# Four graph layers on one core: the row ends of the attention layer on ScalarE, two tiles at a time, between head sums and denominators

## The chip, the cores and the metric

The kernel runs on one core of a Trainium2 chip. The time is the device time of one execution in microseconds, and the time before is the median of three runs. A profile is one further execution, recorded instruction by instruction. Engines are named as the profile names them: PE is TensorE's matmul stream and PEld its weight loads, DVE is VectorE, ACT is ScalarE, POOL is GpSimd, SP is SyncE, whose queue issues most loads.

## The reference, cut to what matters

Four layers follow each other on N = 2708 rows of F = 256 features with one dense matrix adj (2708 x 2708). Each is `x = layernorm(x + layer(x, adj))`. The change concerns the end of layer 1, a graph attention layer with four heads of 64 features:

```python
h = (x @ W).reshape(n, heads, head_dim)
e = src[:, :, None] + dst.T[None, :, :]          # one number per row, head and column
e = jnp.where(e > 0, e, ALPHA * e)
e = jnp.where(adj[:, None, :] > 0, e, NEG_INF)
attn = jax.nn.softmax(e, axis=-1)
out = jnp.einsum('nhm,mhd->nhd', attn, h).reshape(n, heads * head_dim)
mu, var = out.mean(-1), out.var(-1)
out = (out - mu) / jnp.sqrt(var + LN_EPS) * gamma + beta
x = layernorm(x + out)
```

Layer 2 starts from three numbers per row (attention logits of its three heads), a product of the new x with a 256 x 3 matrix. The rest of layer 2 and layer 3 are not touched.

## The kernel before

Rows are held in 22 tiles of 128 (the last has 20). Layer 1 goes through the rows in three groups, each of two segments: 8, 8 and 6 tiles, that is 1024, 1024 and 660 columns of transposed output. A group takes two passes, one for each pair of heads (`q`). A pass is a loop over 22 chunks `c` of 128 rows of the sum. For each chunk VectorE makes two weight tiles `p`, one per head (L665, the exponential of the logits as a maximum of products, times the mask); a pool of four `p` buffers lies between VectorE and TensorE. TensorE then sums on each segment the heads (`heads`, L647, 64-column matmuls of one head beside the other) into `acc`, and the denominators (`totals`, L656, 32-column matmuls) into `den`. Even chunks do heads and then denominators, odd chunks the reverse, so that two equal parts follow each other across a chunk's border. An fp32 matmul shows in the trace as two instructions. At the end of a pass ScalarE copies the two `acc` (L677) and the two halves of `den` (L681) to SBUF; four PSUM banks serve the three that a pass needs, so part of the next pass starts while those copies run.

The row ends of a group run during the two passes of the next one. `layer1_end` turns the sums of one tile into rows (three transposes, L570 and L571), adds beta to x on POOL (L573), divides by the denominators on VectorE (L578, L581, L583), and makes two layer norms with `moments`: bn_stats (L162), bn_aggr (L164), an addition (L166) and a power of -0.5 on POOL (L167), then L590 and L592 between the norms and L595 after the second. `layer1_logits` transposes the new x (L179), copies it to SBUF (L181), stores it through POOL's queue (L602), and multiplies it by the 256 x 3 matrix (L607), which ScalarE copies away (L610). These are generators, and `step(c)`, called at the end of every chunk, advances those begun: in pass 0 a new tile begins about every 2.7 chunks, and goes through the division and the first moments; in pass 1 every second chunk a tile goes through the rest.

The last group has no following passes. Its six row ends are mixed with the first sums of layer 2: `raw_sums` loads adjacency blocks through SP's queue (L256), combines them on VectorE (L296 to L299, and L275 to L278 once), and multiplies them (L309). One step of it follows each of the 13 steps of the row ends. Then come sums of the logits (L722), which need all of `u_all`, in a form that VectorE splits into `u_parts`.

What each engine executes is in order. The order is not simply that of the loops: a planner at build time estimates when each instruction could start, takes the order of the program as priority, and lets later instructions go ahead of ones that it thinks not ready. An instruction that waits on the chip holds up all that are behind it on its engine.

Of the kernel before, what the change touches and what calls it, by code (L numbers as in the profile page):

```python
# [9 lines left out]
F32 = mybir.dt.float32  # L10
# [9 lines left out]
P = 128  # L20
# [7 lines left out]
def kernel(  # L28
# [356 lines left out]
    if True:  # L385
# [13 lines left out]
        if True:  # L399
# [162 lines left out]
            if True:  # L562

                def layer1_end(pool, t, s, sums, dens):

                    n = sz(t)
                    at = (t - [lo for lo, hi in spans if hi > t][0]) * P
                    pt = ps_t.tile([P, 4, P], F32, tag="tr", name="tr")
                    for q in range(H // 2):
                        nc.tensor.transpose(pt[:n, q, :], sums[q][s][:, at : at + n], ident)  # L570
                    nc.tensor.transpose(pt[:n, H // 2, :], dens[s][:, at : at + n], ident)  # L571

                    nc.gpsimd.tensor_tensor(xs[t][:n], xs[t][:n], beta_b[:n], ALU.add)  # L573
                    yield
                    rden = small.tile([P, H // 2, 2], F32, tag="rdenh", name="rdenh")
                    totals = pt[:n, H // 2, :].rearrange("p (q i c) -> p q i c", i=2, c=CT)[:, :, :, CT - 1]
                    if s == 0:
                        nc.vector.reciprocal(rden[:n], totals)  # L578
                    else:
                        for q in range(H // 2):  # L580
                            nc.vector.reciprocal(rden[:n, q], totals[:, q ^ s])  # L581
                    o = pool.tile([P, F], F32, tag="o", name="o", bufs=len(ended))
                    nc.vector.tensor_tensor(  # L583
                        o[:n].rearrange("p (h d) -> p h d", d=HD),
                        pt[:n, : H // 2, :].rearrange("p q (i d) -> p (q i) d", d=HD),
                        rden[:n].rearrange("p q i -> p (q i)")[:, :, None].to_broadcast([n, H, HD]),
                        ALU.mult,
                    )
                    mean, rs = moments(o, n)
                    nc.vector.scalar_tensor_tensor(o[:n], o[:n], mean, gamma_b[:n], ALU.subtract, ALU.mult)  # L590
                    yield
                    nc.vector.scalar_tensor_tensor(o[:n], o[:n], rs, xs[t][:n], ALU.mult, ALU.add)  # L592
                    mean, rs = moments(o, n)
                    yield
                    nc.vector.tensor_scalar(xs[t][:n], o[:n], mean, rs, ALU.subtract, ALU.mult)  # L595

                def layer1_logits(pool, t):

                    n = sz(t)
                    xt = transposed(ps_t, pool, xs[t], n, "xt")  # L600
                    at, _, d = [p for p in xt_d if p[0] <= t * P][-1]
                    nc.gpsimd.dma_start(d[:, :, t * P - at : t * P - at + n], xt[:, :, :n])  # L602
                    yield

                    pm = ps_t.tile([P, 4, P], F32, tag="tr", name="pm")
                    for f in range(FC):
                        nc.tensor.matmul(  # L607
                            pm[:n, 0, :K], xt[:, f, :n], uw[:, f, :], start=(f == 0), stop=(f == FC - 1)
                        )
                    nc.scalar.copy(u_all[:n, t], pm[:n, 0, :K])  # L610
# [4 lines left out]
                for g in range(0, len(spans), 2):  # L615
# [9 lines left out]
                    def step(c):  # L625
# [4 lines left out]
                        if q == 0 and len(halves) < len(ended) and c > len(halves) * 8 // 3:  # L630
# [66 lines left out]
                for k in range(len(ended) + 7):  # L697
                    for i in range(len(ended)):
                        if 0 <= k - i < 4:
                            next(ends[i], None)  # L700
# [771 lines left out]
```

## Time and profile before

| quantity | us |
|---|---|
| median of 3 runs (lowest, highest) | 1925.73 (1924.24, 1928.12) |
| the profiled execution | 1929.04 |
| its span | 1927.3 |
| layer 1, group 1 (1024 columns, no row ends), pass 1 | 60.67 |
| group 2 (1024 columns, row ends of 8 tiles), passes 0 and 1 | 67.16 and 70.87 |
| group 3 (660 columns, row ends of 8 tiles), passes 0 and 1 | 50.05 and 55.27 |
| from there to the logits sums (row ends of 6 tiles) | 50.81 |

The passes are cut where ScalarE's copies of `den` start. A line of a window's answer gives start and end, the length, and then busy time with a count for PE, PEld, DVE, ACT and POOL, the granted clock of TensorE, the share of DMA time and GB/s. A line of a timeline gives start, length, engine, line, operation, written from read tiles, shapes and count, and in brackets how long the engine had been idle and what ended that. A line of the groups gives line, engine, operation and tiles, a count, busy time with the mean of one in ns, and the idle time before. The durations of neighbouring instructions on one engine overlap by up to about 0.1 us, so the distance from start to start is what an instruction costs in a row of them.

### The profile page before, as it was taken

The numbers are of one execution on the slowest core, as the hardware profiler recorded it, in microseconds if no ns is written. First come the engines' busy times: TensorE is split into PE (matmuls) and PEld (weight loads), VectorE is DVE, ScalarE is ACT, GpSimd is POOL, SyncE is SP. The second block draws the span as 40 slices with busy tenths as digits, with TensorE's granted clock in tenths as the row PEclk, the third lists the DMA queues.
The fourth block names the chain that finished last, engine by engine and source line by source line (L and its number), as shares of the span: only waits on it lengthen the run. The fifth ranks groups of instructions, "written<-read, shape, count | busy, mean of one in ns | idle before, by whom it ended". The sixth has DMA issues, their size and how long they took to land.

```text
span 1927.3 us, 22585 instructions
## 1 busy us (share of the span) xinstructions
PE 1864.0 (97%) x7475; PEld 1011.5 (52%) x7479; DVE 1316.4 (68%) x2409; ACT 617.2 (32%) x1064; POOL 261.2 (14%) x435
## 2 busy tenths in 40 slices
PE   8999989999999999999899999999999999999996
PEld 7788832222233778678444444444445555654444
DVE  4334368899898947455557889585877758855665
ACT  4444400000100103111355656455555555311001
POOL 1212110001112421000001000020200101211101
PEclk9999999999999999999999999999999999999998
DMA  8334400000000647555746656454554444643653
GB/s 294 123 143 159 155 23 1 2 28 9 15 1 23 157 103 194 141 131 121 206 137 187 182 163 174 121 158 112 148 155 127 116 114 124 186 115 97 197 152 101
DMA packets 432922, 235.90 MB, mean 122 GB/s; under 512 B 172150, under 2 KB 420620, under 8 KB 430364
## 3 DMA queue, kind: packets, MB, share of 16 engines
q1 hardware_dynamic: 416158, 207.40, 39.2%
q0 software_dynamic: 7760, 21.20, 3.5%
q10 hardware_dynamic: 8878, 5.76, 1.0%
q8 instruction: 62, 1.02, 0.2%
q14 instruction: 64, 0.52, 0.1%
HBM read 221.61 MB, written 12.65 MB: 122 GB/s over the span
## 4 chain that ended last, share of the span: by engine, by line
PE 80%; DMA 6%; DVE 6%; ACT 3%; issue 2%; SPq 2%; POOL 1%; ACTq 0%; DVEq 0%; POOLq 0%
PE m L309 38%; PE acc L647 10%; PE acc L203 7%; PE bank L1007 7%; PE den L656 5%; PE gate L882 4%; PE bank L983 3%; DMA strip<-in_adj_t_dram 2%; DVE p L665 2%; PE bank L1058 2%; SPq L256 1%; ACT below L452 1%; DVE p L1141 1%; PE pm L410 1%; POOL bn_rs L167 1%
## 5 line engine op out<-in xcount | busy, mean ns | idle before, releaser
L665 DVE SCALAR_TENSOR_TENSOR p<-fall_b,rise,mask 128x1024 f32<-128x1024 f32 (+1 forms) x264 | 297.7, 1150 | 27.1 <-PE den L656 14.6
L1137 ACT ACTIVATE p<-st,e_neg 128x1024 f32<-128x1024 f32 (+1 forms) x198 | 197.1, 1040 | 207.8 <-PE m L309 195.4
L309 PE MATMUL m<-s,xq 128*128 128x512 f32 (+3 forms) x660 | 230.3, 467 | 0.0
L647 PE MATMUL acc<-p,h 128*64 128x512 f32 (+2 forms) x1056 | 224.0, 556 | 3.0 <-DVE p L665 2.8
L203 PE MATMUL acc<-turn,strip 128*128 128x257 f32 (+1 forms) x836 | 191.6, 380 | 0.0
L309 PE MATMUL m<-p,xq 128*128 128x512 f32 (+1 forms) x396 | 183.9, 546 | 0.3 <-DVE p L297 0.3
L1140 ACT ACTIVATE p<-p 128x1024 f32<-128x1024 f32 (+1 forms) x198 | 178.8, 943 | 0.2
L309 PE MATMUL m<-p,x 128*128 128x512 f32 (+1 forms) x396 | 169.7, 547 | 5.1 <-DVE p L1141 4.8
L1141 DVE TENSOR_TENSOR p<-p,blk 128x1024 f32<-128x1024 f32 (+1 forms) x132 | 142.5, 1098 | 42.3 <-ACT p L1140 29.9
L296 DVE TENSOR_TENSOR s<-p 128x512 f32<-128x512 f32 (+1 forms) x132 | 83.1, 631 | 120.9 <-PE m L309 101.9
L203 PEld LDWEIGHTS acc<-turn,strip 128*128 128x128 f32 (+1 forms) x836 | 151.5, 185 | 25.3 <-issue 0.5
L309 PEld LDWEIGHTS m<-s,xq 128*128 128x128 f32 x660 | 124.7, 191 | 75.2 <-issue 58.9
L647 PEld LDWEIGHTS acc<-p,h 128*64 128x64 f32 x1056 | 65.5, 136 | 147.8 <-issue 117.5
L167 POOL TENSOR_TENSOR bn_rs<-bn_rs,neg_half 128x1 f32<-128x1 f32 (+1 forms) x110 | 81.8, 745 | 380.1 <-DVE bn_rs L166 373.2
L309 PE MATMUL m<-s,x 128*128 128x512 f32 (+3 forms) x330 | 127.2, 467 | 0.0
L656 PE MATMUL den<-p,h 128*32 128x512 f32 (+2 forms) x1056 | 124.1, 551 | 2.8 <-DVE p L665 2.7
L309 PEld LDWEIGHTS m<-p,x 128*128 128x128 f32 x396 | 74.9, 191 | 79.2 <-issue 61.1
L309 PEld LDWEIGHTS m<-p,xq 128*128 128x128 f32 x396 | 74.5, 190 | 77.8 <-issue 61.2
L452 ACT ACTIVATE below<-strip 128x384 bf16<-128x384 f32 x132 | 78.5, 594 | 72.6 <-DMA strip<-in_adj_t_dram 69.2
L1141 DVE TENSOR_TENSOR p<-p,turn 128x1024 f32<-128x1024 f32 (+1 forms) x66 | 71.6, 1107 | 21.4 <-ACT p L1140 13.3
L681 ACT COPY den<-den 64x512 f32<-64x512 f32 (+2 forms) x12 | 6.3, 529 | 249.2 <-PE den L656 249.1
L297 DVE TENSOR_TENSOR p<-p 128x512 f32<-128x512 f32 (+1 forms) x132 | 83.0, 629 | 1.7
(243 smaller groups left out, 2514.9 us busy)
## 6 DMA issues: line engine op xcount, KB each, us to landing
strip<-in_adj_t_dram SPq DMA_DIRECT2D x19, 1408.0 KB, 6.2
blk<-in_adj_t_dram SPq DMA_DIRECT2D x88, 256.0 KB, 3.4
blk<-in_adj_t_dram SPq DMA_DIRECT2D x88, 192.0 KB, 4.0
pa<-in_adj_t_dram SPq DMA_DIRECT2D x110, 128.0 KB, 2.7
turn<-in_adj_t_dram SPq DMA_DIRECT2D x44, 256.0 KB, 3.1
blk<-in_adj_t_dram SPq DMA_DIRECT2D x88, 128.0 KB, 2.5
p<-in_adj_t_dram SPq DMA_DIRECT2D x44, 256.0 KB, 3.5
turn<-in_adj_t_dram SPq DMA_DIRECT2D x44, 192.0 KB, 3.2
```

Source lines behind the costliest of these rows:

```text
L167: nc.gpsimd.tensor_tensor(rstd[:n], rstd[:n], neg_half[:n], ALU.pow)
L203: nc.tensor.matmul(acc, s[:, c, :n], rhs(c), start=(c == 0), stop=(c == NT - 1))
L296: nc.vector.tensor_tensor(s1, a21, a22, ALU.add)
L309: nc.tensor.matmul(dst[:, :w], lt, rt, start=start and not (one_bank and i), stop=stop and not (one_bank and i in (1, 2, 5)))
L452: nc.scalar.activation(below[:, : (hi - lo) * P], s[:, lo:hi].rearrange("p c n -> p (c n)"), AF.Relu, scale=-1.0, accum_out=negative[:, BE ...
L647: nc.tensor.matmul(acc[s][i * HD : (i + 1) * HD, :ws], hs[c][:, 2 * q + i, :HD], ps[i][:, p0 : p0 + ws], **flags,)
L656: nc.tensor.matmul(den[j : j + CT, :ws], hs[c][:, 2 * q + i, HD + 1 - CT :], ps[i][:, p0 : p0 + ws], **flags,)
L665: nc.vector.scalar_tensor_tensor(p[:, :w], falls[g // 2][:, 2 * q + i, :w], rise[:, c, 2 * q + i : 2 * q + i + 1], mask[:, c, at : at + w] ...
L1007: nc.tensor.matmul(g[:, :w], lt, rt, start=(q == 0), stop=(q == len(terms) - 1))
L1137: nc.scalar.activation(p[:, :, :w], st_k[:, :, :w], AF.Relu, scale=-1.0, bias=e_neg[:, at, k : k + 1])
L1140: nc.scalar.activation(p[:, :, :w], p[:, :, :w], AF.Exp, scale=-1.0)
L1141: nc.vector.tensor_tensor(p[:, :, :w], p[:, :, :w], blk[:, i, :, :w], ALU.mult)
```

## The change

- `layer1_end` takes two tiles at once. Division, means and variances are made on ScalarE: four copies of 64 columns from PSUM, scaled by the reciprocal, each with a sum of its outputs; a fifth adds these to the mean; a Square with a sum of its outputs gives the variance. VectorE keeps the reciprocals, one addition and multiplication per pair before the power (`power`, with POOL's power of both tiles in one instruction), and two scalar_tensor_tensor per tile between the norms, the second of which also gives the sum for the second mean. The last normalization is a ScalarE Identity with scale and bias.
- There are more and longer steps: two of a pair's steps do nothing, so that two chunks lie between a variance's last operand and its use.
- `layer1_logits` takes two tiles at once: four transposes into one bank, one copy, two stores; then eight (as seen in the trace) matmul instructions and one copy.
- Rows `o`, the discarded output of Square and the transposed x lie in `turn`, whose contents (x before layer 0) are no longer needed, instead of in buffers of their own.
- In the passes, even chunks do denominators and then heads, odd chunks the reverse. `step(c)` is called between the two parts instead of after them. `den` is allocated before `acc`.
- The pool of `p` has six buffers instead of four.
- In the tail, three pairs go through ten steps each, begun one step apart: 12 steps, each with one of `raw_sums`, instead of 13.

```diff
-                def layer1_end(pool, t, s, sums, dens):
...
+                def variance(o, mean, var, n):
+                    nc.scalar.activation(
+                        turn[:n, 2 * GT * F : (2 * GT + 1) * F], o[:n], AF.Square, bias=mean, accum_out=var
+                    )
+                def power(pool, pair, var):
+                    rs = pool.tile([P, 2], F32, tag="o_rs", name="o_rs", bufs=12)
+                    for v, r in zip(halves_of(pair, var), halves_of(pair, rs)):
+                        nc.vector.tensor_scalar(v, v, 1.0 / F, EPS, ALU.mult, ALU.add)
+                        nc.gpsimd.tensor_tensor(r, v, neg_half[: v.shape[0]].to_broadcast(list(v.shape)), ALU.pow)
+                    return rs
+                def layer1_end(pool, pair):
...
+                    for t, s, sums, dens, row in pair:
...
+                        for q in range(H // 2):
+                            nc.tensor.transpose(pt[:n, q, :], sums[q][s][:, at : at + n], ident)
+                        nc.tensor.transpose(pt[:n, H // 2, :], dens[s][:, at : at + n], ident)
+                        pts.append(pt)
+                        nc.gpsimd.tensor_tensor(xs[t][:n], xs[t][:n], beta_b[:n], ALU.add)
+                    yield
+                    for i, (t, s, sums, dens, row) in enumerate(pair):
...
+                        for h in range(H):
+                            nc.scalar.activation(
+                                o[:n, h * HD : (h + 1) * HD], pt[:n, h // 2, h % 2 * HD : (h % 2 + 1) * HD], AF.Copy,
+                                scale=rden[:n, h // 2, h % 2 : h % 2 + 1], accum_out=parts[:n, h : h + 1],
+                            )
+                        nc.scalar.activation(
+                            parts[:n], parts[:n], AF.Copy, scale=-1.0 / F, accum_out=mean[:n, i : i + 1]
+                        )
+                        variance(o, mean[:n, i : i + 1], var[:n, i : i + 1], n)
+                    yield
+                    rs = power(pool, pair, var)
+                    yield
+                    yield
+                    for i, (t, s, sums, dens, row) in enumerate(pair):
...
+                        nc.vector.scalar_tensor_tensor(
+                            o[:n], o[:n], mean[:n, i : i + 1], gamma_b[:n], ALU.add, ALU.mult
+                        )
+                        nc.vector.scalar_tensor_tensor(
+                            o[:n], o[:n], rs[:n, i : i + 1], xs[t][:n], ALU.mult, ALU.add,
+                            accum_out=mean2[:n, i : i + 1],
+                        )
+                        nc.scalar.mul(mean2[:n, i : i + 1], mean2[:n, i : i + 1], -1.0 / F)
+                        variance(o, mean2[:n, i : i + 1], var2[:n, i : i + 1], n)
+                    yield
+                    rs2 = power(pool, pair, var2)
+                    yield
+                    yield
+                    for i, (t, s, sums, dens, row) in enumerate(pair):
...
+                        nc.scalar.mul(mean2[:n, i : i + 1], mean2[:n, i : i + 1], rs2[:n, i : i + 1])
+                        nc.scalar.activation(
+                            xs[t][:n], o[:n], AF.Identity, scale=rs2[:n, i : i + 1], bias=mean2[:n, i : i + 1]
+                        )
+                def layer1_logits(pair):
...
+                            nc.tensor.transpose(pt[:, i * FC + f, :n], xs[t][:n, f * P : (f + 1) * P], ident[:n, :n])
+                    if all(sz(a[0]) == P for a in pair):
+                        nc.scalar.copy(xt.rearrange("p i f n -> p (i f) n"), pt)
...
+                        nc.gpsimd.dma_start(d[:, :, t * P - at : t * P - at + n], xt[:, i, :, :n])
                     yield
...
+                        nc.scalar.copy(u_all[:, pair[0][0] : pair[0][0] + 2], pm[:, :2, :K])
...
-                        if q == 0 and len(halves) < len(ended) and c > len(halves) * 8 // 3:
-                            halves.append(layer1_end(l1, *ended[len(halves)]))
+                        if q == 0 and c % 5 == 1 and len(halves) < len(ended):
+                            halves.append(layer1_end(l1, ended[len(halves)]))
+                            next(halves[-1])
                             steps.append(itertools.islice(halves[-1], 2))
+                        if q == 1 and c % 5 == 0 and c // 5 < len(halves):
+                            steps.append(itertools.chain(halves[c // 5], [None], layer1_logits(ended[c // 5])))
                             next(steps[-1])
...
+                        den = ps_acc.tile([P, W], F32, tag="acc", name="den")
                         acc = [ps_acc.tile([P, W], F32, tag="acc", name="acc") for _ in segs]
-                        den = ps_acc.tile([P, W], F32, tag="acc", name="den")
...
-                                p = l1.tile([P, 2 * W], F32, tag="p", name="p", bufs=4)
+                                p = l1.tile([P, 2 * W], F32, tag="p", name="p", bufs=6)
...
-                            for part in (heads, totals)[:: 1 if c % 2 == 0 else -1]:
+                            for part in (heads, totals)[:: -1 if c % 2 == 0 else 1]:
                                 part(c, ps, dict(start=(c == 0), stop=(c == NT - 1)))
-                            step(c)
+                                if part is (totals, heads)[c % 2]:
+                                    step(c)
...
-                for k in range(len(ended) + 7):
...
+                turns = [itertools.chain(layer1_end(tail, a), [None], layer1_logits(a)) for a in ended]
+                k = 0
+                while turns:
+                    for a in turns[: k + 1]:
+                        if next(a, a) is a:
+                            turns.remove(a)
+                            k -= 1
                     next(ahead)
+                    k += 1
```

## The prediction

> **What bounds the kernel now.** I read the page's totals first, then the stages of layer 1 as windows, then TensorE's timeline inside them, then the waits there.
>
> ```profile
> span 1927.3 us, 22585 instructions
> PE 1864.0 (97%) x7475; PEld 1011.5 (52%) x7479; DVE 1316.4 (68%) x2409; ACT 617.2 (32%) x1064; POOL 261.2 (14%) x435
> ```
>
> TensorE is busy nearly always, so a gain must take TensorE instructions out, make them denser, or remove its small waits. The copies of den on ScalarE end the six passes of layer 1 (L665 to L681) at 324.50, 385.17, 452.33, 523.20, 573.25 and 628.52 us. Cut there (columns: window, length, then busy time of PE, PEld, DVE, ACT, POOL, each with its count, then PE clock, DMA share and GB/s):
>
> ```profile
> 324.50:385.17 60.67, 60.67 (x354) 14.29 (x356) 54.51 (x45) 2.33 (x4) 0.00 (x0) 1.00 0.00 1
> 385.17:452.33 67.16, 66.53 (x378) 17.39 (x379) 63.88 (x94) 2.23 (x4) 4.60 (x7) 1.00 0.07 21
> 452.33:523.20 70.87, 69.76 (x402) 20.07 (x402) 64.10 (x89) 6.61 (x20) 16.45 (x17) 1.00 0.05 16
> 523.20:573.25 50.05, 49.40 (x378) 17.12 (x379) 46.99 (x94) 2.23 (x5) 4.84 (x7) 1.00 0.01 1
> 573.25:628.52 55.27, 51.02 (x402) 20.92 (x402) 47.37 (x90) 5.89 (x21) 13.13 (x26) 1.00 0.07 20
> ```
>
> The first line is a pass without row ends: 22 chunks in 60.67 us, 5.515 per two. The other four carry the row ends of eight tiles each and cost more: 6.5 and 10.2 us over that pass at full width. VectorE is busy 86 to 95% there, ScalarE under 11%. TensorE's timeline in the narrow passes (start, length, instructions, idle before and releaser):
>
> ```profile
> 585.69 0.84 PE L656 MATMUL den<-p,h 128*32 128x384 f32 x8
> 586.46 0.44 PE L179 MATMUL tr<-ident,x 128*128 128x128 f32 x2
> 587.41 0.61 PE L607 MATMUL pm<-uw,xt 128*128 128x3 f32 x4 [0.51 <-ACT xt L181]
> 587.95 0.84 PE L656 MATMUL den<-p,h 128*32 128x384 f32 x8
> 588.72 2.44 PE L647 MATMUL acc<-p,h 128*64 128x384 f32 x16
> 591.09 0.84 PE L656 MATMUL den<-p,h 128*32 128x384 f32 x8
> ...
> 623.01 1.49 PE L656 MATMUL den<-p,h 128*32 128x384 f32 x16
> 624.43 2.60 PE L647 MATMUL acc<-p,h 128*64 128x384 f32 x16
> 626.95 1.48 PE L656 MATMUL den<-p,h 128*32 128x384 f32 x16
> ```
>
> From one den run to the one two chunks on takes 626.95-623.01 = 3.94 us bare, 43.3 us a pass, but 591.09-585.69 = 5.40 with one tile's logits. So the narrow passes carry 6.7 and 12.0 us of row ends. Of the 1.46 us, 0.37 are transposes, 0.51 a wait for ScalarE's xt copy, 0.54 the logits.
>
> At full width, a tile's three transposes in the first pass lengthen two chunks from 5.515 to 6.07 (starts 390.65 and 396.72): 0.55 us, of which 0.08 is the break in the acc run. In the second pass the period is 6.63 (489.15 to 495.79): 1.12 us, of which 0.14 is the den run's break (1.00+1.00 against 1.86) and 0.08 the acc run's. A tightly packed set of seven transposes took 0.91 us:
>
> ```profile
> 426.55 0.33 PE L570 MATMUL tr<-ident,sum 128*128 128x128 f32 x1
> ...
> 427.46 1.07 PE L656 MATMUL den<-p,h 128*32 128x512 f32 x8
> ```
>
> **What the Trainium skill says.** The page TensorEngine Tiling, section Key Properties: "Changing tiling mode (not just tile) drains the TensorE". The trace agrees: a 128-column transpose within a run of 32- or 64-column matmuls costs 0.14 or 0.08 us beside its own time. The page ScalarE: Activation LUTs, section What ACT_TABLE_LOAD costs, gives 186 ns + 0.833 ns per column for an ACTIVATE, about 93 ns per pointer operand, about 93 ns overlap; for L1178 (256 columns, two pointers) that is 585, and the trace has 600. The same page prices a switch of function tables at about 2.7 us; the trace has a single load of 1.28 us. Whether Square needs one no row shows; I take none, and two (there and back) would lie in ScalarE's idle time of passes of 50 to 70 us. The rows I price with:
>
> ```profile
> L452 ACT ACTIVATION_READ_ACCUMULATOR below<-strip 128x1 f32 x132 | 24.6, 187 | 0.0
> L181 ACT COPY xt<-tr 128x256 f32<-128x256 f32 x42 | 15.5, 369 | 110.7 <-PE tr L179 103.2 <-issue 6.7 <-DMA xt<-xt 0.6
> L1178 ACT ACTIVATE o<-o,bn_mv,bn_rs 128x256 f32<-128x256 f32 x21 | 12.6, 600 | 64.7 <-DVE bn_mv L1177 62.7 <-DMA out_dram<-o 2.0
> ```
>
> **The change part by part.**
>
> *VectorE.* By the starts in its timeline, a tile gives up L583 (0.33), both L162/L164/L166 groups (2 x 0.49) and L595 (0.33): 1.64 us, and the 0.46 us for which each L595 waits for POOL. It keeps reciprocals (0.1 to 0.2) and two L590/L592 forms (0.39 each, read here for the new accumulating one too). The two power steps add 0.06 each per pair. A pair falls from about 6.0 us (2 x (1.64+0.46+0.1+0.78)) to 2.0 (0.3+4 x 0.39+2 x 0.06). A p costs 0.81 to 0.83 us back to back in the narrow passes, 1.66 a chunk, so VectorE has 36.5 us of p in a pass of 43.3: after the change it is not the limit by load.
>
> *TensorE.* Instructions stay equal in number; the places fall from six per pair to three, each at the border of acc and den, where the mode changes anyway. A pair's six sum transposes: 0.8 us (0.91 x 6/7), before 1.10. Its four xt transposes 0.5 and eight logits instructions 1.0 (0.54 x 2 less a common start): 1.5, before 2.24. With four pairs a pass:
> - full width, first pass: 60.67+3.2 = 63.9, before 67.2: -3.3
> - full width, second: 60.67+6.0 = 66.7, before 70.9: -4.2
> - narrow, first: 43.3+3.2 = 46.5, before 50.1: -3.5
> - narrow, second: 43.3+6.0 = 49.3, before 55.3: -6.0 (the 0.51 us waits go, because copy and logits now lie a step apart)
>
> Sum -17.0. The first two passes carry no row ends and stay. Both ends of this sum: were the instructions put mid-run again, each of the 12 places per pair of passes (three per pair, four pairs) would cost 0.08 to 0.14 more, 24 x 0.1 = 2.4 in all; were they free apart from their own time, nothing more than the -17 is there.
>
> *ScalarE.* First step, per tile: four 64-column copies with a scale pointer, 186+53+93 = 332 by the page, 187 for the accumulator, less overlap, 0.43 each, 1.7; mean 0.35; Square 0.5 to 0.6. That is 2.6 a tile, 5.2 a pair. Later: two muls 0.3, Squares 1.3, finals about 1.2, copies 0.8. About 9 us a pair, 36 a pair of passes that last 131 or 96: hidden under TensorE. What is not hidden is latency: VectorE's first power step waits for 5.2 us of ScalarE, and TensorE's xt transposes wait for the finals. Bounds: 0, if p's are queued ahead of the waiting instruction (six p buffers allow three chunks of lead), up to the rival's 15 us below. I take 0.3 us a pair and pass pair, 8 x 0.3 = +2.4.
>
> *Pass borders.* Den is now allocated first and finished last, so a pass's first acc reuses the bank of the den before. Den ends, then both den copies run, 1.2 us plus about 0.2 of signal, partly behind the acc copies; meanwhile TensorE has the next den part of 0.93. About 0.5 us is left, before 0.16. Five borders, +2.0, bounds 0 to 3.5.
>
> *POOL and DMA.* POOL's pow falls from one per tile to one per pair, beta adds and xt stores stay in number (two per pair, behind one copy); SP's queue is not passed. Nothing waits for the stores in layer 1 but the reuse of the xt rows two pairs later: zero, hidden behind ten chunks.
>
> *Tail* (628.52 to 679.33, 50.8 us, PE 46.95 busy). Twelve steps of raw sums instead of 13 now lie before the logits sums; the step is done later at the same 2.68 us. Its SP queue issues about 97 loads from 629.85 to 684, so dropping a step helps a little and freeing VectorE (45.3 of 50.8) takes two 0.5 us waits away. Against that, last logits to u_parts have one step as cover instead of two. I take -1, bounds -4 to +4.
>
> Sum: -17.0+2.4+2.0-1.0 = -13.6 on a profiled execution of 1929.04 us (span 1927.3), that is 1915.4; the runs' median is 3.3 lower, 1925.73-13.6 = 1912.
>
> **Rivals.** *More is gained*: no handoff costs, borders hidden, tail -4: -21, 1905. For it: ScalarE idles 90%. Against: L595's repeated 0.46 us waits show that the order does not foresee such latencies exactly.
>
> *Handoffs eat half.* ScalarE is priced too short by the order; VectorE and TensorE each wait about 0.5 us per pair and pass (16 x 0.5 = 8 instead of 2.4), and the borders cost 3.5: -17+8+3.5-1 = -6.5, 1919. Waits of 0.51 and 0.46 at L607 and L595 speak for it, the free p buffers against.
>
> *Slower: VectorE is blocked at the first power step.* If it keeps loop order, only p(c+2) lies between the reciprocals and the wait. Counted from the transposes in chunk c, ScalarE is done at 0.5+5.2 = 5.7; p(c+3) then ends at 7.4 in narrow passes, where TensorE wants it at 2.5 x 1.96 = 4.9: 2.5 us lost per pair; at full width 8.1 against 6.9: 1.2. Four pairs each: 15 us. With the finals 0.5 us late for eight pairs, +4, the sum is -17+15+4+2 = +4, and 2 to 3 more if ScalarE takes 6 us: 1932. It decides once the chain of 5.2 us is not overtaken by p(c+3). For it: everything behind on VectorE is p, which TensorE needs. Against: in the trace p's do slip between L162, L164 and L166, so the order is not the loop's.
>
> *No difference*: merging at borders is undone by the order and gains and handoffs cancel: 1925.
>
> **How the numbers follow.** Chances: forecast (1906 to 1918) 0.52, handoffs (1918 to 1922) 0.20, more gained (1896 to 1906) 0.11, no difference 0.05, slower 0.12. A measurement here tells about 0.2%, 3.9 us. Faster 0.83, same 0.05, slower 0.12. The range 1903 to 1924 leaves out the slower case and over half of the large gain.
>
> **What would show it.** Right: the four passes with row ends at about 64, 67, 47 and 49 us; transposes only between acc and den runs; no wait of the logits instructions for their copy; VectorE busy below 90% in them; ACTIVATE rows near 330 and 500 ns with 187 for the accumulator. Wrong: idle on VectorE before the power step for ScalarE's Square, followed by TensorE waiting for p; TensorE waiting for xs; borders over 1 us; a tail longer than 51 us.

## The result and the profile after

| | before | after |
|---|---|---|
| median, four runs each (us) | 1925.79 (1924.24 to 1928.12) | 1900.83 (1899.13 to 1902.43) |
| ratio, 95% interval | | 0.9869 [0.9857, 0.9881] |
| the profiled execution, its span | 1929.04, 1927.3 | 1902.43, 1900.7 |
| layer 1, from its first matmul to the one that follows its last | 365.7 (263.92 to 629.63) | 344.9 (262.52 to 607.39) |
| tail, to the first logits sum | 49.6 | 45.3 |
| logits sums to the end of the last store's issue | 1241.7 | 1243.6 |
| from there to the end of the span | 6.3 | 4.4 |

The change makes the kernel 25 us faster, 1.3%. The forecast was 13.6 us, and 1900.83 lies below its range. In the two profiled executions layer 1 also begins 1.4 us earlier after the change; the change touches nothing before it, and among the kernels below, the two with added copies left out, this beginning varies by some 3 us. The totals of the changed kernel's page:

```profile
PE 1848.4 (97%) x7475; PEld 1024.5 (54%) x7479; DVE 1283.9 (68%) x2279; ACT 689.6 (36%) x1418; POOL 249.6 (13%) x415
```

TensorE executes the same 7475 instructions in 15.6 us less busy time. VectorE lost 130 instructions and ScalarE gained 354. The changed kernel in windows, as before (pass 1 of group 1, then passes 0 and 1 of groups 2 and 3). The cuts stand at the starts of the den runs that span the borders, because ScalarE's own work now delays some of the den copies by which the passes before were cut:

```profile
324.50:384.32 59.82, 59.82 (x354) 16.25 (x353) 54.58 (x45) 2.33 (x4) 0.00 (x0) 1.00 0.05 15
384.32:447.36 63.04, 63.04 (x378) 18.81 (x376) 60.58 (x86) 25.90 (x128) 8.45 (x7) 1.00 0.03 9
447.36:513.47 66.11, 66.11 (x402) 21.81 (x401) 54.49 (x48) 10.04 (x26) 6.35 (x9) 1.00 0.05 17
513.47:558.56 45.09, 45.09 (x377) 20.49 (x377) 42.22 (x79) 22.15 (x117) 5.17 (x5) 1.00 0.01 1
558.56:606.62 48.06, 47.82 (x402) 23.64 (x400) 37.73 (x55) 11.98 (x36) 10.07 (x20) 1.00 0.07 23
```

The length and the PE busy time are equal in four of the five: TensorE has no gap left there. The first line is the surprise. That pass has no row ends in either kernel, and it went from 60.67 to 59.82 us although PE was already busy for all of it before. The other four shrank by 4.1, 4.8, 5.0 and 7.2. These five add up to 21.9 us, the layer as a whole to 20.8, although its first pass, which is not in the list, has the shorter period too.

What is missing lies at the beginning of layer 1, where TensorE runs at a granted clock of 0.50 in both kernels, for different times. The first 12 us from the first matmul, before and after:

```profile
263.92:275.92 12.00, 12.00 (x62) 2.96 (x64) 9.35 (x8) 0.00 (x0) 0.00 (x0) 0.88 0.00 1
...
262.52:274.52 12.00, 12.00 (x52) 3.08 (x54) 10.27 (x9) 0.00 (x0) 0.00 (x0) 0.74 0.00 1
```

The mean clock of 0.88 and 0.74 stands for 2.9 and 6.2 us at 0.50. At 0.50 a matmul takes twice as long: the first den part of the changed kernel takes 1.86 us from start to start, and later two of them take 1.85. So the two beginnings cost about 1.5 and 3.1 us. In the fourteen profiles of this case this loss lies between 1.5 and 3.1 us. Without it layer 1 takes 364.2 us before and 341.8 after, and the change is worth 22.4 us there.

TensorE's timeline of the changed kernel, narrow passes:

```profile
517.48 0.44 PE L595 MATMUL tr<-ident,sum 128*128 128x128 f32 x2
517.76 0.27 PE L596 MATMUL tr<-ident,den 128*128 128x128 f32 x1
517.87 0.38 PE L595 MATMUL tr<-ident,sum 128*128 128x128 f32 x2
518.08 0.27 PE L596 MATMUL tr<-ident,den 128*128 128x128 f32 x1
518.29 1.49 PE L727 MATMUL den<-p,h 128*32 128x384 f32 x16
519.70 2.44 PE L718 MATMUL acc<-p,h 128*64 128x384 f32 x16
522.07 1.49 PE L727 MATMUL den<-p,h 128*32 128x384 f32 x16
...
567.68 2.44 PE L718 MATMUL acc<-p,h 128*64 128x384 f32 x16
570.06 0.66 PE L657 MATMUL tr<-ident,x 128*128 128x128 f32 x4
570.64 1.48 PE L727 MATMUL den<-p,h 128*32 128x384 f32 x16
572.06 1.05 PE L674 MATMUL pm<-uw,turn 128*128 128x3 f32 x8
573.04 2.44 PE L718 MATMUL acc<-p,h 128*64 128x384 f32 x16
```

The row ends stand where the change puts them: no run of 16 is broken, and the logits instructions no longer wait for their copy. A pair's sums take 518.29-517.48 = 0.81 us; its logits add 0.58 and 0.98. And again the surprise: with nothing between, two chunks take 522.07-518.29 = 3.78 us, where they took 3.94.

Waits over the whole run (engine and line that waited, the one waited for, total us, times, longest), in the kernel before:

```profile
PEld den L656 <- DVE p L665: 25.9, 36, 1.5
...
PEld acc L647 <- DVE p L665: 23.8, 32, 2.8
```

and in the changed kernel:

```profile
PEld den L727 <- DVE p L736: 3.7, 4, 2.8
...
PEld acc L718 <- DVE p L736: 2.0, 7, 0.3
...
DVE o_var L580 <- ACT turn L572: 1.6, 2, 1.4
```

Before, TensorE's weight loads waited 68 times for a `p`; now 11 times. (What is loaded are columns of h, 64 or 32 of them; `p`, up to 512 columns, is the other operand of the matmul. The trace shows the wait for `p` on the load all the same.) The last line is the handoff that the prediction charged for: VectorE's power step waits for ScalarE's Square twice in all.

In the pass without row ends alone, before, there are 22 such waits; after, none:

```profile
PEld acc L647 <- DVE p L665: 8.0, 11, 0.7
PEld den L656 <- DVE p L665: 7.7, 11, 0.8
```

VectorE was not too slow for this pass: it waited 23 times itself, 6.5 us in all, until TensorE gave a buffer free. In this pass each waited for the other. What one such wait does is seen in the weight loads themselves, before:

```profile
327.96 0.16 PEld L656 LDWEIGHTS den<-p,h 128*32 128x32 f32 x8 [0.81 <-issue]
328.88 0.16 PEld L656 LDWEIGHTS den<-p,h 128*32 128x32 f32 x8 [0.76 <-DVE p L665]
329.88 0.20 PEld L647 LDWEIGHTS acc<-p,h 128*64 128x64 f32 x4 [0.84 <-issue]
...
331.62 0.20 PEld L647 LDWEIGHTS acc<-p,h 128*64 128x64 f32 x4 [0.69 <-DVE p L665]
```

and after:

```profile
329.93 0.16 PEld L727 LDWEIGHTS den<-p,h 128*32 128x32 f32 x8 [0.81 <-issue]
330.39 0.13 PEld L727 LDWEIGHTS den<-p,h 128*32 128x32 f32 x4 [0.30 <-issue]
330.82 0.13 PEld L727 LDWEIGHTS den<-p,h 128*32 128x32 f32 x4 [0.30 <-issue]
331.79 0.20 PEld L718 LDWEIGHTS acc<-p,h 128*64 128x64 f32 x4 [0.84 <-issue]
```

Before, the loads for the second chunk of a run start when its `p` arrives; after, they follow each other evenly. The PE row shows no gap in either. The page TensorE: Matmul & The Clock Gate of the Trainium skill, section Step-by-step: what each phase is for, says that weight loads can be pulled ahead of running matmuls. That fits: a load that waits for its `p` cannot be pulled ahead. The trace does not show what happens inside the array.

### The profile page after: what moved, and what is told of

The parts are those of the page before. It is cut to its first block, busy times and chain, and to the rows that moved or that the text cites. A ratio compares the mean times of both kernels' runs of the same rounds, so it can differ in the third digit from the quotient of the medians.

```text
span 1900.7 us, 22827 instructions
## 1 busy us (share of the span) xinstructions
PE 1848.4 (97%) x7475; PEld 1024.5 (54%) x7479; DVE 1283.9 (68%) x2279; ACT 689.6 (36%) x1418; POOL 249.6 (13%) x415
## 4 chain that ended last, share of the span: by engine, by line
PE 85%; DVE 4%; DMA 4%; issue 2%; ACT 2%; POOL 1%; SPq 1%; ACTq 0%; DVEq 0%; POOLq 0%
PE m L309 39%; PE acc L718 11%; PE acc L203 8%; PE bank L1083 7%; PE den L727 6%; PE gate L958 4%; PE bank L1059 3%; PE bank L1134 2%; PE acc L510 1%; POOL bn_rs L167 1%; DMA strip<-in_adj_t_dram 1%; PE pm L410 1%; DVE p L1217 1%; SPq L256 1%; DMA blk<-in_adj_t_dram 1%
## 5 line engine op out<-in xcount | busy, mean ns | idle before, releaser
L736 DVE SCALAR_TENSOR_TENSOR p<-fall_b,rise,mask 128x1024 f32<-128x1024 f32 (+1 forms) x264 | 293.1, 1155 | 34.7 <-PE den L727 17.8
L718 PE MATMUL acc<-p,h 128*64 128x512 f32 (+2 forms) x1056 | 216.6, 553 | 0.2 <-ACT sum L749 0.2
L718 PEld LDWEIGHTS acc<-p,h 128*64 128x64 f32 x1056 | 70.5, 137 | 140.9 <-issue 131.7
L727 PE MATMUL den<-p,h 128*32 128x512 f32 (+2 forms) x1056 | 118.2, 551 | 2.6 <-DVE p L736 2.6
L299 DVE TENSOR_TENSOR s<-p,s 128x512 f32<-128x512 f32 (+1 forms) x132 | 83.0, 629 | 2.0
L309 PEld LDWEIGHTS m<-s,x 128*128 128x128 f32 x330 | 61.7, 190 | 38.4 <-issue 34.1
```

The source lines that it names most:

```text
L299: nc.vector.tensor_tensor(s4, a12, s2, ALU.subtract)
L309: nc.tensor.matmul(dst[:, :w], lt, rt, start=start and not (one_bank and i), stop=stop and not (one_bank and i in (1, 2, 5)))
L718: nc.tensor.matmul(acc[s][i * HD : (i + 1) * HD, :ws], hs[c][:, 2 * q + i, :HD], ps[i][:, p0 : p0 + ws], **flags,)
L727: nc.tensor.matmul(den[j : j + CT, :ws], hs[c][:, 2 * q + i, HD + 1 - CT :], ps[i][:, p0 : p0 + ws], **flags,)
L736: nc.vector.scalar_tensor_tensor(p[:, :w], falls[g // 2][:, 2 * q + i, :w], rise[:, c, 2 * q + i : 2 * q + i + 1], mask[:, c, at : at + w] ...
```

## The experiments

The theory after the result, called **buffers** here: VectorE delivered `p` just in time with four buffers, every such arrival cost TensorE a little that its busy row hides, and the two more buffers account for the part that the forecast missed. Its rivals: the **order** at the border (the transposes' place, and den first) saved more than priced; the **load** taken from VectorE did; and, for what lies outside layer 1, a **shift** of one `raw_sums` step from the tail into layer 2. In the lengths below layer 1 is taken from its first matmul to the one that follows its last, in one profiled execution. Kernels whose layer 1 is the same in all that matters agree within 0.7 us: 365.7, 366.3 and 366.3 for before, b_turn and b_12, 344.9, 344.5 and 344.2 for the changed kernel, a_13 and a_short. Without the loss at the clock of 0.50 they agree within 0.1: 364.2 for each of the first three, 341.8 for each of the others. Where such a length is given below, it is called the length at full clock.

**Buffers taken out of the changed kernel (a_p4), put into the kernel before (b_p6), and their control (b_turn).** To make room, b_p6 also moves the rows `o` and the transposed x into `turn`, as the change does; b_turn makes that move alone, with four buffers.

```diff
# a_p4, against the changed kernel
-  p = l1.tile([P, 2 * W], F32, tag="p", name="p", bufs=6)
+  p = l1.tile([P, 2 * W], F32, tag="p", name="p", bufs=4)
# b_p6, against the kernel before; b_turn without the last edit
-  o = pool.tile([P, F], F32, tag="o", name="o", bufs=len(ended))
+  o = turn[:, t % (2 * GT) * F : (t % (2 * GT) + 1) * F]
-  xt = transposed(ps_t, pool, xs[t], n, "xt")
+  ...  # the same transposes and copy, into two rows of turn
-  p = l1.tile([P, 2 * W], F32, tag="p", name="p", bufs=4)
+  p = l1.tile([P, 2 * W], F32, tag="p", name="p", bufs=6)
```

> The changed kernel with four p buffers instead of six, all else kept. Theory 'buffers': in the profile of before, two bare chunks take 5.515 us at 1024 columns and 3.94 at 660, in the changed kernel 5.44 and 3.79, because weight loads on TensorE no longer wait for p; four passes x 11 x 0.075 + two passes x 11 x 0.155 = 6.7 us. So with four buffers the periods return and it is 6 to 9 us slower than the changed kernel, about 1908. Rival 'order': the shorter period comes from the order of den and acc runs; then it stays within 2 us, 1901 to 1903.

> The kernel before with six p buffers instead of four (rows o and the transposed x moved into the free tile turn to make room, nothing else). Theory 'buffers': the bare periods fall to 5.44 and 3.79 us, 6.7 us; and where VectorE is late in the narrow pass 0 some of 2 to 3 us go too: 1916 to 1920. Rival 'order': no more than 2 us, 1924 to 1926. Rival 'VectorE's load': buffers can't help where VectorE has no spare time, so the narrow passes stay at 50 and 55 us.

> The kernel before with rows o and the transposed x in the free tile turn, and four p buffers: what b_p6 has beside its buffers. Theory 'buffers': nothing moves, the passes stay at 60.67, 67.2, 70.9, 50.1 and 55.3 us (each within 0.5), so that b_p6's gain is the buffers' alone. Rival: the moved rows free a wait and give 2 us or more of b_p6's gain.

Measured: a_p4 1911.71 us, 0.992 [0.9903, 0.9936], which is 9.8 us slower than the changed kernel by the ratios, a little more than the 6 to 9 expected; its layer 1 takes 353.5. b_p6 1916.94, 0.9946 [0.9929, 0.9962], 10.4 us faster than before; layer 1 357.7. b_turn, a single execution without an interval, 1927.43, layer 1 366.3, with the passes of before to 0.01 us (60.67, 67.16, 70.87, 50.04, 55.27). The waits of a_p4, whole run:

```profile
PEld den L727 <- DVE p L736: 35.6, 56, 2.8
...
PEld acc L718 <- DVE p L736: 31.0, 53, 0.9
```

and of b_p6:

```profile
PEld acc L652 <- DVE p L670: 3.7, 5, 2.8
PEld den L661 <- DVE p L670: 2.7, 7, 1.3
```

Two buffers bring the waits back or take them away, in either kernel, and the pass without row ends follows: 60.72 us in a_p4, 59.82 in b_p6. So the buffers are worth about 10 us of time, 8.0 to 8.6 of it in layer 1 (8.9 in b_p6 and 8.8 in a_p4 at full clock), whatever the row ends look like. The rival, that they do nothing in the changed kernel because VectorE has less to do there, is refuted. The recorded rival that the narrow passes of b_p6 stay at 50 and 55 us was half right: the first fell to 47.2, but the second hardly gained, 54.85 against 55.27. What it waits for shows next.

**The order alone, and with the buffers (b_border, b_border_p6).** Both keep the row ends of before.

```diff
-  acc = [ps_acc.tile([P, W], F32, tag="acc", name="acc") for _ in segs]
   den = ps_acc.tile([P, W], F32, tag="acc", name="den")
+  acc = [ps_acc.tile([P, W], F32, tag="acc", name="acc") for _ in segs]
...
-  for part in (heads, totals)[:: 1 if c % 2 == 0 else -1]:
+  for part in (heads, totals)[:: -1 if c % 2 == 0 else 1]:
...
-  step(c)
+      if part is (totals, heads)[c % 2]:
+          step(c)
```

> The kernel before with the order of the change alone: even chunks den then acc, odd chunks the reverse, the step of the row ends between the two parts, den allocated first; single tiles, moments on VectorE, four p buffers. Theory 'places': 48 places in the four passes save about 0.1 us each, 5 us, and a part of the eight waits of 0.5 us between xt copy and logits may go: 1917 to 1921. Rival 'load': VectorE's row ends set these passes, then less than 2 us: 1924 to 1926.

> The kernel before with both the order of the change and six p buffers; row ends still single and on VectorE. Theory 'places and buffers': the two add up, 11 to 16 us, 1910 to 1915, so that most of the change's 25 us needs neither pairs nor ScalarE. Rival 'load': without VectorE's relief six buffers fill but do not stay full, and it gains less than 8 us: 1918 or more.

Measured: b_border 1922.1, 0.9975 [0.9965, 0.9985], a gain of 4.8 us that is just short of what was expected; layer 1 362.4. b_border_p6 1915.24 (1912.82 to 1917.09), 0.9943 [0.9926, 0.9959]; layer 1 351.1. By the profiles the order saves 3.3 us of layer 1 with four buffers and 6.6 with six (4.6 and 6.3 at full clock). The medians don't resolve this second step: -10.4 us for b_p6, -11.0 for b_border_p6, with intervals that overlap. A large part of it is the wait of the logits instructions for the copy of x. It stands seven times, 3.5 us, in the second narrow pass of before and of b_p6; TensorE's timeline of b_p6:

```profile
593.12 0.44 PE L602 MATMUL tr<-ident,x 128*128 128x128 f32 x2
594.06 0.61 PE L612 MATMUL pm<-uw,turn 128*128 128x3 f32 x4 [0.51 <-ACT turn L605]
594.60 0.84 PE L661 MATMUL den<-p,h 128*32 128x384 f32 x8
```

In the new order a part of the chunk stands between the transposes and the logits, and the wait is gone from both kernels; in b_border_p6:

```profile
580.13 0.41 PE L602 MATMUL tr<-ident,x 128*128 128x128 f32 x2
580.47 1.33 PE L652 MATMUL acc<-p,h 128*64 128x384 f32 x8
581.74 0.61 PE L612 MATMUL pm<-uw,turn 128*128 128x3 f32 x4
```

That pass takes 52.4 us in b_border and 51.2 in b_border_p6, where it took 55.3 and 54.85 without the order.

**Where the step is called (a_stepend).** The changed kernel with `step(c)` after both parts, as before.

```diff
-  if part is (totals, heads)[c % 2]:
-      step(c)
+  step(c)    # after the loop over the parts
```

> The changed kernel with the step of the row ends after both parts of a chunk, as before, all else kept: transposes and logits now split runs of equal parts. Theory 'places': 24 places x about 0.1 us = 2.4 us slower, 1903 to 1904. Rival: the order of the other engines moves too and waits come back, 5 us or more, 1906.

Measured: 1905.51, 0.9887 [0.987, 0.9903]. That is 3.5 us above the changed kernel by the ratios, with intervals that overlap; layer 1 346.0, 1.1 longer, and the tail 0.8. At full clock layer 1 is 2.0 longer, near the 2.4 that the theory of the places had; the time lies between the two expectations. What else lies in the 3.5 us was not traced.

**ScalarE taken out again (a_dve).** Pairs, steps, order and six buffers stay; the division, the moments and the last normalization go back to VectorE and POOL.

```diff
-  for h in range(H):
-      nc.scalar.activation(o[...], pt[...], AF.Copy, scale=rden[...], accum_out=parts[...])
-  nc.scalar.activation(parts[:n], parts[:n], AF.Copy, scale=-1.0 / F, accum_out=mean[...])
-  variance(o, mean[...], var[...], n)
+  nc.vector.tensor_tensor(o[...], pt[...], rden[...].to_broadcast([n, H, HD]), ALU.mult)
+  mean, rs = moments(o, n)
...
-  nc.scalar.activation(xs[t][:n], o[:n], AF.Identity, scale=rs2[...], bias=mean2[...])
+  nc.vector.tensor_scalar(xs[t][:n], o[:n], *second[i], ALU.subtract, ALU.mult)
```

> The changed kernel with division, moments and last normalization back on VectorE and POOL (the forms of before), in pairs, with the steps, order and six buffers of the change. Theory 'TensorE sets the passes': VectorE's load rises by about 1.6 us a tile, 26 us over the four passes, but it has 0.3 us spare per chunk (26 us) and six buffers; full-width passes stay, narrow ones lose a little: 0 to 5 us slower, 1901 to 1906. Rival 'load': the move to ScalarE is what pays, then most of 25 us is lost, 1915 or more.

Measured: 1910.1 (1906.15 to 1911.78), 0.9905 [0.9886, 0.9923]: 6.9 us above the changed kernel, more than expected, and below the 1915 from which the load theory began. Layer 1 is 347.0, 2.1 longer; the tail 2.5 longer; and 2.1 us more lie after the last store. So the move to ScalarE, which makes up most of the diff's text, is worth about 2 us of the 20.8 in layer 1 (2.8 of 22.4 at full clock). In a_dve a few transposes still fall inside a run, as in its timeline here:

```profile
582.26 0.84 PE L713 MATMUL den<-p,h 128*32 128x384 f32 x8
583.03 0.65 PE L643 MATMUL tr<-ident,x 128*128 128x128 f32 x4
583.61 0.84 PE L713 MATMUL den<-p,h 128*32 128x384 f32 x8
```

**The longer steps (a_short).** The changed kernel without its two empty steps per pair; the tail then has ten steps.

```diff
   rs = power(pool, pair, var)
   yield
-  yield
...
   rs2 = power(pool, pair, var2)
   yield
-  yield
```

> The changed kernel without the two empty steps of a pair: the rows between the norms follow the first power at the next step, the last normalization follows the second power at the next. Theory 'the order absorbs it': since the planner moves p's past waiting instructions and six buffers hold three chunks, the passes grow by less than 1 us each: 1900 to 1904. Rival 'handoffs': waits for ScalarE and POOL show up on VectorE and TensorE, 0.5 us or more per pair and pass, 4 us or more: 1905 to 1910.

Measured: 1903.84, 0.9878 [0.9861, 0.9894]; layer 1 344.2, tail 40.9. The longer steps make no difference that can be measured; layer 1 at full clock is the same to 0.1 us, so the built order takes care of the latencies there without them.

**The number of `raw_sums` steps (a_13, b_12).** One more step before the logits sums in the changed kernel, one less in the kernel before.

```diff
# a_13, behind the tail's loop
+  next(ahead)
# b_12, in the tail's loop
-  next(ahead)
+  if k < len(ended) + 6:
+      next(ahead)
```

> The changed kernel with one more step of raw sums before the logits sums, 13 as in the kernel before. Theory 'shift': the tail of 45.3 us grows by 2.7 to 4 and the later phase of gates gives the step back: 0 to 1.5 us slower, 1901 to 1902. Rival 'real gain in the tail': 3 to 4 us slower, 1904 to 1905.

> The kernel before with 12 steps of raw sums before the logits sums instead of 13. Theory 'shift': logits sums start about 3 us earlier, the whole is within 1.5 us, 1924 to 1926. Rival 'real gain in the tail': 3 to 4 us faster, 1922.

Measured: a_13 1901.91, 0.9863 [0.9846, 0.988]; b_12 1928.68, 1.0003 [0.9995, 1.0012]. Neither differs from its parent, though the stages move. The start of the logits sums, in the changed kernel:

```profile
652.71 8.50 PE L798 MATMUL pu<-mask,u_parts 128*32 128x512 fp8e4 x132
```

and in a_13, where they start 5.9 us later and the rest of the run is 4.1 us shorter:

```profile
658.62 8.50 PE L799 MATMUL pu<-mask,u_parts 128*32 128x512 fp8e4 x132
```

A step left out of the tail is done later at the same price. With 13 steps the tail takes 49.2 us in a_13, and from 48.4 to 49.7 in the kernel before and those made from it: at equal work no gain is seen.

**The end of the span (b_pad, a_pad).** The last store comes nearly 2 us closer to the end in all kernels with the row ends on ScalarE. One idea was that the end depends on the number of instructions ScalarE has gone through. So both kernels got added work, 352 copies of one column on ScalarE that nothing uses, meant for the first two passes of layer 1.

```diff
+  pad = const.tile([P, 1], F32, name="pad")
...
+  if g == 0:
+      for _ in range(8):
+          nc.scalar.copy(pad, neg_half)
```

> The kernel before with 352 copies of one column on ScalarE added in the first two passes, where it idles. From the last output store to the end of the span it takes 6.3 us in every kernel with row ends on VectorE and 4.4 in every kernel with them on ScalarE. Theory 'place of the code': that time depends on how many instructions stand before the end, ScalarE's count (354 more in the change) among them: the end falls to 4.4 us, the rest stays: span 1925. Rival: it depends on something else of the row ends: 6.3 us, span 1927.

> The changed kernel with the same 352 copies on ScalarE in the first two passes. Theory 'place of the code': the end may go back to about 6.3 us; rival: 4.4 us as in the changed kernel. The passes stay as they are either way, since ScalarE idles there.

Measured in one execution each: b_pad 1945.16 and a_pad 1916.86. In both the copies were hoisted to between 17 and 130 us, into layer 0, and both kernels take some 15 to 17 us longer than without them. The times therefore say nothing, but the ends do: from the end of the last store's issue it is 6.6 us in b_pad and 4.2 in a_pad, as without the copies (6.3 and 4.4). A count of ScalarE's instructions is not what sets the end.

The traces show where the difference lies. In every kernel POOL's last long instruction is a DRAIN of 4.39 us, and the span ends about 1 us behind it. A line gives the shortest, median and longest in ns, then the first and the last start; before:

```profile
L1468 POOLq DRAIN  x3: 50/106/4392, 1922.0 to 1927.0; - x3
```

and after:

```profile
L1544 POOLq DRAIN  x3: 50/107/4392, 1895.2 to 1900.4; - x3
```

Before, it begins 1.0 us after the last store's issue has ended (1921.0), in the changed kernel 1.1 before that (1896.3). Ahead of it POOL executes a branch and then a semaphore instruction; between their starts lie 2.5 us before, from 1919.4 to 1921.9, and 0.5 after, from 1894.7 to 1895.2. All kernels divide in the same way: the DRAIN begins 1.0 to 1.5 us after the store where the row ends are on VectorE, and 1.1 before it where they are on ScalarE. The same kernels differ in POOL's instructions, 435 against 415, which the copies on ScalarE left as they were. What POOL does in the 2.5 us, the traces do not name, and no run changes POOL's instructions alone, so the cause stays open.

**The steps put together.** Each row adds one part to the row above it:

| kernel | layer 1 | step | at full clock | step | ratio to before | whole time, step |
|---|---|---|---|---|---|---|
| before | 365.7 | | 364.2 | | 1 | |
| six buffers (b_p6) | 357.7 | -8.0 | 355.3 | -8.9 | 0.9946 [0.9929, 0.9962] | -10.4 |
| and the order (b_border_p6) | 351.1 | -6.6 | 349.0 | -6.3 | 0.9943 [0.9926, 0.9959] | -0.6 |
| and pairs, longer steps, 12 in the tail (a_dve) | 347.0 | -4.1 | 344.6 | -4.4 | 0.9905 [0.9886, 0.9923] | -7.3 |
| and ScalarE (after) | 344.9 | -2.1 | 341.8 | -2.8 | 0.9869 [0.9857, 0.9881] | -6.9 |

Each ratio is uncertain by some 2 to 4 us, so the last column is rough, the middle rows above all; the columns of layer 1 are sharper, but of one execution each. The row of the pairs changes three things at once; the steps' length (a_short) and their number (a_13, b_12) made no difference that can be measured, so what is left for this row are the pairs, which no run tests alone. None of the experiments is measurably faster than the changed kernel.

## Why the prediction was right or wrong

In layer 1 the forecast had -12.6 us and the runs show -20.8. Three of its terms failed: the base from which the passes were priced, and the charges for handoffs and borders.

*The sum over the four passes: -17.0, measured -21.1.* The step that failed is its base: "60.67+3.2" and "43.3+3.2" take the bare periods of 5.515 and 3.94 us for TensorE's own pace. They were not. PE was shown busy throughout, VectorE at 90% (54.51 of 60.67 us), and I read this as TensorE being the limit with VectorE close behind. The wait that told otherwise was in the profile: the 22 waits of that pass shown above, once in every run of two parts. With six buffers the periods are 5.44 and 3.785, 0.83 us less in a full pass and 1.7 in a narrow one. The six buffers, which I counted only as cover for handoffs, were the largest single part.

*The prices on top of the base* held. I charged 3.2, 6.0, 3.2 and 6.0 us for the row ends of the four passes; over the new bare passes they are 63.04-59.82 = 3.2, 6.3, 45.09-41.6 = 3.5 and 6.4. The transposes and logits went to the borders of the runs, as foreseen, and cost what a packed group cost before. The 0.51 us waits of the logits went too; b_border shows that the new order alone is enough for that, without a step more between copy and logits.

*"The first two passes carry no row ends and stay"* failed for the same reason: pass 1 of group 1 gained 0.85 us, and the lengths at full clock say the same of pass 0.

*VectorE was named "not the limit by load"*, and as a sign of it less than 90% busy in the four passes. That sign held in two of them (82 and 79%) and failed in the two first passes of groups 2 and 3 (60.58 of 63.04 us, 96%, and 42.22 of 45.09, 94%). TensorE was busy throughout there and the prices held all the same (3.2 and 3.5 us against 3.2), so with six buffers the busy VectorE cost nothing that shows.

*Handoffs, +2.4: none found.* The prices of ScalarE's instructions were about right, as the groups of the four passes show (total busy us, mean ns, then the idle time before them):

```profile
L613 ACT ACTIVATE turn<-tr,rdenh 128x64 f32<-128x64 f32 x64 | 19.6, 321 | 23.0 <-DVE rdenh L609 13.8 <-DVE rdenh L606 9.2
L572 ACT ACTIVATE turn<-turn,o_mean 128x256 f32<-128x256 f32 x32 | 16.4, 512 | 0.7
L613 ACT ACTIVATION_READ_ACCUMULATOR turn<-tr,rdenh 128x1 f32 x64 | 13.6, 213 | 0.0
```

The estimate from the Trainium skill's page ScalarE: Activation LUTs, section What ACT_TABLE_LOAD costs, was 332 ns for the first row, measured 321; for a Square of 256 columns with one pointer operand the estimate is 186+213+93 = 492, measured 512. The accumulator's read took 213 where I put 187. But the chain was priced too long: in six of the eight pairs it takes 4.1 us from the first copy to the end of the second Square (390.75 to 394.87 in the first), not 5.2, because the scaled copies begin every 0.29 us and not every 0.43. In the other two it runs together with later steps. The power steps on VectorE stand late enough to be met by these results: of the two waits shown above, 0.16 us fall into the four passes and 1.4 into the tail. The rival in which VectorE is blocked there, 2.5 us per pair in narrow passes, did not occur. It needed the instructions to keep the order of the loops; even without the empty steps (a_short) no such loss shows.

*Borders, +2.0: none found.* I let the first acc of a pass wait for the bank of the den before. TensorE's timeline at a border after the change:

```profile
324.50 1.92 PE L727 MATMUL den<-p,h 128*32 128x512 f32 x16
326.35 3.65 PE L718 MATMUL acc<-p,h 128*64 128x512 f32 x16
329.94 1.92 PE L727 MATMUL den<-p,h 128*32 128x512 f32 x16
```

and ScalarE's copies there:

```profile
325.66 1.17 ACT L753 COPY den<-den 64x512 f32<-64x512 f32 x2 [0.46 <-PE den L727]
```

The acc run starts at its usual distance of 1.85 us while the den copies still run until 326.83. So its first matmuls do not wait for that bank. I had inferred from the order of allocation that they reuse it; which of the four banks they are given no trace shows.

*Tail, -1: measured -4.3 for it alone, of which -2.4 is net once layer 2 is counted.* The rest was moved, not saved, as a_13 and b_12 show. From the start of the logits sums to the last store the changed kernel takes 1.9 us longer. After the last store it takes 1.9 less, in a stretch that the prediction left out; the difference is POOL's, as shown above. So outside layer 1 about 4.3 us were gained against 1 forecast, and only the 1.9 at the end stand clear of the scatter. The remaining 2 us do not: at 13 steps, from the first logits sum to the last store, a_13 takes 1239.5 us, and the kernel before and b_turn, which are alike there, take 1241.7 and 1239.3.

*The rivals.* "More is gained", with its handoffs free and borders hidden, had the right two terms and was put at 1905; it too lacked the buffers. Its tail of -4 agrees with the -4.3 by luck: it stood for a saving, and most of the -4.3 came back in layer 2 or does not stand clear of the scatter. In the balance of layer 1, -12.6 forecast against -20.8 measured: 4.4 us are the handoffs and borders, 4.1 the shorter passes with row ends, and 1.7 the two without; the longer time at a clock of 0.50 takes 1.6 back, and the rest of 0.3 is the different cuts.

## What to carry to other kernels

A PE row that is busy for the whole of a window does not prove that TensorE sets the pace: look at what its weight loads wait for, and compare the period with one in which nothing is late. When the producer is about 90% busy and delivers just in time, try more buffers first; here two, in memory that another tile no longer needed, brought about 10 of the 25 us. Where lengths of a stage are compared between executions, look at the granted clock at its beginning first: here it moves them by up to 1.6 us. And work that is moved past the last point of a stage should be priced in the stage where it comes back.

## What was not expected of the hardware

- A moving operand that arrives just in time costs TensorE time that its busy row doesn't show: 5.515 against 5.44 us per two chunks of 512 columns (four parts), 3.94 against 3.785 at 660 columns in two segments. It follows the waits of the weight loads, which two more buffers removed in both kernels (68 to 12 in b_p6, 109 to 11 between a_p4 and the changed kernel). The mechanism inside the array is not shown.
- Between the issue of the last store and the end of the span lie 6.2 to 6.7 us in the kernel before and all kernels with row ends on VectorE, 4.2 to 4.6 in all with row ends on ScalarE. The difference lies on POOL, whose DRAIN of 4.39 us begins 1.0 us or more after the last store's issue in the former and 1.1 us before its end in the latter. The number of ScalarE's instructions isn't the cause.
- At the beginning of layer 1 TensorE's granted clock is 0.50 for 2.9 to 6.2 us, depending on the execution. Without this, kernels with the same layer 1 agree within 0.1 us.
